# Two feed-forward stages of a four-layer gated transformer: bfloat16 terms without GpSimd, an integer layer's bias as a matrix product, and its rounding issued before attention's last tile

## The chip, the cores and the metric

The kernel runs on one core of a Trainium2 chip. The core has five engines, which run side by side and wait for each other through semaphores: TensorE (PE; its weight loads are shown apart as PEld), VectorE (DVE), ScalarE (ACT), GpSimd (POOL) and SyncE (SP), which here only issues DMAs. Data lies in SBUF, and matrix products arrive in PSUM.

The metric is the device time of one execution, in microseconds, as the median of several. A profile is one such execution with a record of every instruction. Its span is the time from the first instruction to the last.

## The reference

The input x has 4 x 256 tokens of 256 features. Four layers follow each other, each with an attention over a context of 64 rows and a feed-forward part. Either part adds `tanh(gate) * f(layernorm(x))` to x. The two feed-forward parts that matter here are those of layers 1 and 2:

```python
def _L1_ffn_ref(x, w1, b1, w2, b2):
    w1_q = absmean_quant(w1)                    # values -1, 0, 1
    w2_q = absmean_quant(w2)
    h = jnp.einsum('bsd,fd->bsf', x, w1_q) + b1           # 256 -> 1024
    h = jax.nn.gelu(h, approximate=False)
    out = jnp.einsum('bsf,df->bsd', h, w2_q) + b2         # 1024 -> 256
    return out

def _L2_ffn_ref(x, weight, bias):
    w_max = jnp.clip(jnp.max(jnp.abs(weight), axis=1, keepdims=True), 1e-08, None)
    w_scale = w_max / QMAX                                # QMAX = 127
    w_q = jnp.clip(jnp.round(weight / w_scale), QMIN, QMAX).astype(jnp.int8)
    w_scale = w_scale.squeeze(1).astype(jnp.float32)
    x_max = jnp.max(jnp.abs(x), axis=2, keepdims=True)
    x_scale = jnp.maximum(x_max / QMAX, 1e-12)
    x_q = jnp.clip(jnp.round(x / x_scale), QMIN, QMAX).astype(jnp.int8)
    acc = jnp.einsum('bnd,od->bno', x_q.astype(jnp.int32), w_q.astype(jnp.int32))
    y = acc.astype(jnp.float32) * x_scale.astype(jnp.float32) * w_scale[None, None, :]
    y = y + bias
    return y.astype(x.dtype)
```

Layers 0 and 3 have mixtures of experts as their feed-forward parts, and the attentions differ from layer to layer.

## The kernel before

The 1024 tokens are 8 tiles of 128 (`NT`), taken in 2 groups of 4 (`NG`, `TPG`). A group's 512 tokens are one moving operand of a product. x stays in SBUF for the whole kernel, as `stream`, with one view `x[t]` a tile. Eight steps run in order: attention and feed-forward of layer 0, then 1, 2 and 3.

The code issues instructions to the five engines, and each engine works its own list in order. The lists aren't quite in the order of the code. When the program is built, a scheduler puts an instruction forward that would be ready earlier by its own reckoning, and takes the order of the code as priority. In the trace, VectorE clears a tile of the last step (L1002) at 695.74 us, while attention of layer 2 still runs. So moving a call in the code moves its priority, and only with it its place.

Buffers come from pools by tag. PSUM has four single-bank tiles (`ps_mm`, tag `mm`) and two double ones (`ps_wide`). Of the normalised tiles (tag `xn`) there are six, which attention's small context copies share.

**Layer 1's feed-forward** (`ffn1`, L1518). The weights are -1, 0 and 1 and exact in bfloat16. The activations are split into three bfloat16 terms whose sum is the float32 value, so each product is done three times in bfloat16. `inputs(g)` (L1524) normalises a group, transposes it and makes its terms, with two casts on ScalarE (L1535, L1537) and two subtractions on VectorE (L1536, L1538) for each half of the features. `up(g)` (L1543) goes through four blocks `f2` of 256 hidden features: 12 products (L1553), two Gelus on ScalarE (L1560), and then `three_terms` (L1479), which splits the block's 128 x 1024 values into three terms. Its four instructions are a cast on ScalarE (L1481), a subtraction on GpSimd (L1482), a cast on VectorE (L1483) and a subtraction on VectorE (L1484). The inputs of group 1 are made ahead of block 2 of group 0. `down(g)` (L1564) takes the terms of all four blocks: 24 products a tile (L1569), the bias (L1577), and the add into x (L456). `in_turn` (L472) issues up 0, up 1, down 0, down 1.

**Layer 2's weights** (`weights2`, L1586) are rounded and transposed before `ffn1` is issued, into `wqT`, 512 columns of a tile with the tag `hits`, which nothing else uses. The gate is multiplied into them there.

**Attention of layers 2 and 3** (`attention23`, L887) runs through `in_flight` (L458), a pipeline of 11 turns over the 8 tiles. In turn i it first lets a side job (`beside`) do one step, then issues the scores of tile i, the add into x of tile i - 3 (`gated_add`, L455), the softmax weights of tile i - 1 (`weights`, L431, a GpSimd multiply), and the attend of tile i - 2 (transposes L451, their evacuations L452, products L953, a context copy L962, products L965). In layer 2 (`keyed`, L974) the side job prepares layer 3's keys and values.

**Layer 2's feed-forward** (`ffn2`, L1613) first loads the bias to all 128 partitions through GpSimd's queue and multiplies the gate into it on GpSimd (L1617). For each group there follow: `layernorm` with the normalisation on ScalarE (statistics L379 and L380, Sqrt L382, normalisation L391), the bias added into the group's four tiles of x on GpSimd (L1622), the largest absolute value of each row (L1626), scale and its inverse (L1627, L1628), rounding to whole numbers on VectorE (L1631, L1632), `transposed` (L400: transposes L406, evacuations L132 and L134), and for each tile two products with `wqT` (L1637) and the add of the product times the row's scale (L456).

`ROUND` is 1.5 x 2^23: adding and subtracting it rounds a float32 to a whole number.

Of the kernel before, what the change touches and what calls it, by code (L numbers as in the profile page):

```python
# [28 lines left out]
F32 = mybir.dt.float32  # L29
# [5 lines left out]
ALU = mybir.AluOpType  # L35
AX = mybir.AxisListType

P = 128
B, S, D = 4, 256, 256
T = B * S  # L40
NT = T // P
TH = 512
NG = T // TH
TPG = TH // P
# [8 lines left out]
ROUND = 12582912.0  # L53
# [28 lines left out]
def tile_flamingo(ctx: ExitStack, tc: tile.TileContext, a: dict, out: bass.AP):  # L82
# [7 lines left out]
    def ps_mm():  # L90
        return psum.tile([P, 512], F32, tag="mm", name="mm", bufs=4)
# [7 lines left out]
    def region(tag, cols, name):  # L99
        return sb.tile([P, cols], F32, tag=tag, name=name, bufs=1)  # L100
# [21 lines left out]
    def small(shape, name, bufs=3):  # L122
        return sb.tile(shape, F32, tag=name, name=name, bufs=bufs)
# [29 lines left out]
    def output_bias(name, src):  # L153

        c = const.tile([P, D], F32, tag="b2", name=name)
        nc.gpsimd.dma_start(out=c[: src.shape[0]], in_=src)
        return c
# [297 lines left out]
    def gated_add(t, ps, gate):  # L455
        nc.vector.scalar_tensor_tensor(x[t], ps, gate, x[t], ALU.mult, ALU.add)  # L456
# [430 lines left out]
    def attention23(layer, gate, beside):  # L887
# [83 lines left out]
        if layer == 3:  # L971
            used("L3")

    def keyed(layer, gate):  # L974
        beside = iter(())
        if layer == 2:
            values = region("wqk", 2048, "values")
            for _ in keys_values(2, region("weff", 2048, "kbd2"), values[:, :1024]):
                pass
            beside = keys_values(3, region("wvo", 2048, "kbd3"), values[:, 1024:])  # L980
        attention23(layer, gate, beside)
        for _ in beside:
            pass
# [492 lines left out]

        return loaded[f"L1_w{k}"][:, :1024].bitcast(BF16)

    def three_terms(terms, v, rest):  # L1479

        nc.scalar.copy(terms[0], v)  # L1481
        nc.gpsimd.tensor_tensor(rest, v, terms[0], ALU.subtract)  # L1482
        nc.vector.tensor_copy(terms[1], rest)  # L1483
        nc.vector.tensor_tensor(terms[2], rest, terms[1], ALU.subtract)  # L1484

    def ternary1():
# [31 lines left out]
    def ffn1(gate):  # L1518
# [23 lines left out]

        def up(g):  # L1543
            for f2 in range(4):
                if g == 0 and f2 == 2:
                    xT.append(inputs(1))
                h = t4([P, 2, TH], "h")
                for j in range(2):
                    f = 2 * f2 + j
                    ps = ps_mm()  # L1550
                    for k, term in enumerate(xT[g]):
                        for c in range(2):
                            nc.tensor.matmul(  # L1553
                                ps,
                                w1[:, c, f * P : (f + 1) * P],
                                term[:, c, :],
                                start=(k == 0 and c == 0),
                                stop=(k == 2 and c == 1),
                            )
                    nc.scalar.activation(h[:, j, :], ps, AF.Gelu, bias=b1_1[:, f : f + 1])  # L1560
                three_terms([hidden[:, g, k, 2 * f2 : 2 * f2 + 2, :] for k in range(3)], h, h)
            return hidden[:, g]

        def down(g, terms):  # L1564
# [21 lines left out]
    def weights2(gate):  # L1586
# [13 lines left out]
            nc.vector.tensor_scalar(q, q, ROUND, 127.0, ALU.subtract, ALU.min)  # L1600
            nc.vector.tensor_scalar(q, q, -128.0, ws[:, c : c + 1], ALU.max, ALU.mult)
        nc.vector.tensor_scalar(wq, wq, gate, None, ALU.mult)
        wqT = sb.tile([P, 768], F32, tag="hits", name="wqT", bufs=1)[:, :512].rearrange("p (d o) -> p d o", d=2)
        ps = ps_mm()
        for d in range(2):
            for c in range(2):
# [1 line left out]
                    ps[:, d * D + c * P : d * D + (c + 1) * P], wq[:, c, d * P : (d + 1) * P], ident  # L1608
                )
        nc.scalar.copy(wqT.rearrange("p d o -> p (d o)"), ps)  # L1610
        return wqT

    def ffn2(gate):  # L1613
        bias_2 = output_bias("bias_2", a["L2_bias"].partition_broadcast(P))
        used("L2")
        wqT = kept.pop("weights2")
        nc.gpsimd.tensor_tensor(bias_2, bias_2, gate.to_broadcast([P, D]), ALU.mult)  # L1617
        for g in range(NG):
            xn = layernorm(g, True)

            tiles = stream[:, g * TPG : (g + 1) * TPG, :]
            nc.gpsimd.tensor_tensor(tiles, tiles, bias_2.unsqueeze(1).to_broadcast([P, TPG, D]), ALU.add)  # L1622
            xs = small([P, TPG], "xs")
            xi = small([P, TPG], "xi")
            for i, n in enumerate(xn):
                nc.vector.tensor_reduce(xs[:, i : i + 1], n, AX.X, ALU.max, apply_absolute_value=True)  # L1626
            nc.vector.tensor_scalar(xs, xs, 1.0 / 127.0, 1e-12, ALU.mult, ALU.max)  # L1627
            nc.vector.reciprocal(xi, xs)  # L1628
            for i, n in enumerate(xn):

                nc.vector.tensor_scalar(n, n, xi[:, i : i + 1], 127.0, ALU.mult, ALU.min)  # L1631
                nc.vector.tensor_scalar(n, n, ROUND, ROUND, ALU.add, ALU.subtract)  # L1632
            xqT = transposed(xn)
            for i in range(TPG):
                ps = ps_mm()
                for d in range(2):
                    nc.tensor.matmul(  # L1637
                        ps[:, :D], xqT[:, d, i * P : (i + 1) * P], wqT[:, d, :], start=(d == 0), stop=(d == 1)
                    )
                gated_add(g * TPG + i, ps[:, :D], xs[:, i : i + 1])  # L1640

    steps = [
        attention0,
# [156 lines left out]
```

## Time and profile before

| | |
|---|---|
| median of 3 runs | 962.89 us (954.0 to 962.95) |
| the profiled execution | 967.09 us |
| its span, first to last instruction | 965.3 us |
| granted TensorE clock, mean over the span | 0.941 |
| attention of layer 1 ends, layer 1's feed-forward begins on TensorE (L1533) | 575.4 us |
| its products up (L1553) | 576.73 to 610.38 us |
| its products down (L1569) | 610.38 to 632.42 us |
| attention of layer 2, its last product (L965) ends | 704.30 us |
| products of layer 2's feed-forward (L1637) | 711.21 to 724.08 us |

Two notes on reading. An instruction's line is that of the helper that issues it: every add into x is L456, whatever stage it belongs to, and only the time tells them apart. A float32 product appears as two records, a bfloat16 one as one. In the timeline, a number in brackets is the idle time of the engine ahead of a row, with the instruction that ended it.

### The profile page before, as it was taken

How to read it: one execution, taken by the hardware profiler on the slowest of the kernel's cores; microseconds unless marked ns; L12 is line 12 of the kernel's file. 1: busy time of each engine (PE TensorE's matmuls, PEld its weight loads, DVE VectorE, ACT ScalarE, POOL GpSimd, SP SyncE). 2: the span in 40 equal slices, each digit the busy share in tenths (PEclk: the TensorE clock that was granted, in tenths of full speed). 3: DMA queues.
4: the chain of work that ended last, by engine and by line, in shares of the span. 5: the costliest groups of instructions: out<-in, count | busy, mean ns of one | idle time of the engine just before them, and what ended most of it. 6: DMA issues, size and time to landing. Idle time of an engine off the chain costs nothing.

```text
span 965.3 us, 12724 instructions
## 1 busy us (share of the span) xinstructions
PE 856.9 (89%) x4467; PEld 555.5 (58%) x4467; DVE 509.9 (53%) x1299; ACT 286.8 (30%) x559; POOL 345.7 (36%) x262
## 2 busy tenths in 40 slices
PE   6999999999999999986199986997867889999994
PEld 4444336876667876764046872754544556666662
DVE  4566648748624444571427755867776856222220
ACT  2122014433112322322113445415534441122221
POOL 1454543110146787786001323402311302144421
PEclk9999999999779999998599999986988999999998
DMA  9201157000256666655640000360000012122223
GB/s 364 79 21 34 61 160 200 22 22 9 84 129 158 125 141 150 121 82 63 186 174 1 1 1 0 111 227 1 1 22 1 1 44 54 43 45 45 39 23 66
DMA packets 38762, 75.15 MB, mean 78 GB/s; under 512 B 6240, under 2 KB 26706, under 8 KB 37322
## 3 DMA queue, kind: packets, MB, share of 16 engines
q1 hardware_dynamic: 23562, 52.01, 16.0%
q0 software_dynamic: 14496, 20.47, 13.1%
q10 hardware_dynamic: 640, 1.84, 0.5%
q8 instruction: 39, 0.64, 0.3%
q14 instruction: 25, 0.20, 0.1%
HBM read 58.73 MB, written 16.61 MB: 78 GB/s over the span
## 4 chain that ended last, share of the span: by engine, by line
PE 31%; DVE 10%; issue 4%; ACT 3%; POOL 2%; DMA 0%; POOLq 0%; ACTq 0%; DVEq 0%
PE wide L1226 7%; PE mm L421 5%; PE mm L1250 3%; PE wide L1436 2%; PE mm L451 2%; PE mm L656 2%; PE mm L965 2%; PE wide L923 1%; PE mm L1457 1%; DVE mx L934 1%; DVE attn L936 1%; PE mm L1637 1%; PE mm L1241 1%; DVE big L1483 1%; POOL h L1482 1%
## 5 line engine op out<-in xcount | busy, mean ns | idle before, releaser
L437 POOL TENSOR_TENSOR attn<-attn,sm 128x1024 f32<-128x1024 f32 x32 | 60.9, 1903 | 212.5 <-DVE sm L436 192.5
L1235 DVE SCALAR_TENSOR_TENSOR blk<-wide,weight,blk 128x176 f32<-128x176 f32 (+1 forms) x75 | 37.0, 493 | 135.3 <-ACT blk L1234 121.2
L1262 POOL DMA_INDIRECT sums<-ring,big x55 | 88.1, 1601 | 33.6 <-issue 10.2
L421 PE MATMUL wide<-xT,big 128*128 128x512 f32 x192 | 86.7, 600 | 0.3 <-ACT big L556 0.3
L683 DVE TENSOR_TENSOR rope<-wide,big 128x512 f32<-128x512 f32 x96 | 59.6, 683 | 47.7 <-PE wide L421 46.6
L1174 POOL DMA_INDIRECT xs<-xd,big x55 | 54.9, 999 | 63.3 <-DMA sums<-x 35.6
L1215 PE MATMUL wide<-big,blk 128*128 x220 | 77.1, 472 | 0.0
L1226 PE MATMUL wide<-big,blk 128*128 x160 | 72.2, 593 | 0.5 <-DVE blk L1187 0.5
L1234 ACT ACTIVATE blk<-wide 128x176 f32<-128x176 f32 (+1 forms) x75 | 29.4, 392 | 122.3 <-PE wide L1226 60.2
L421 PEld LDWEIGHTS wide<-xT,big 128*128 128x128 f32 x192 | 35.0, 190 | 46.7 <-issue 40.5
L656 PE MATMUL mm<-vo,attnT 128*128 128x256 f32 x256 | 59.5, 386 | 0.9 <-ACT attnT L452 0.9
L1250 PE MATMUL mm<-big,blk 88*128 x220 | 57.4, 383 | 0.6 <-ACT blk L1243 0.5
L406 PE MATMUL mm<-ident,xn 128*128 128x128 f32 x112 | 19.4, 320 | 41.6 <-DVE xn L394 35.5
L656 PEld LDWEIGHTS mm<-vo,attnT 128*128 128x128 f32 x256 | 48.0, 193 | 9.1 <-ACT attnT L452 3.1
L456 DVE SCALAR_TENSOR_TENSOR x<-mm,tg,x 128x256 f32<-128x256 f32 x48 | 22.9, 478 | 54.9 <-PE mm L656 17.3
L1250 PEld LDWEIGHTS mm<-big,blk 88*128 88x128 f32 x220 | 41.9, 192 | 16.5 <-ACT blk L1243 1.5
L452 ACT COPY attnT<-mm 128x512 f32<-128x512 f32 x64 | 35.0, 588 | 54.6 <-PE mm L451 54.3
L1215 PEld LDWEIGHTS wide<-big,blk 128*128 128x128 f32 x220 | 40.6, 196 | 13.2 <-issue 1.3
L451 PE MATMUL mm<-ident,attn 128*128 128x128 f32 x256 | 38.0, 297 | 9.9 <-POOL attn L437 9.9
L435 DVE TENSOR_REDUCE sm<-attn 128x16 f32<-128x1024 f32 x32 | 38.8, 1212 | 14.9 <-ACT attn L429 12.4
L1174 POOL DMA_INDIRECT xs<-xd,scratch x20 | 19.5, 976 | 74.6 <-PE mm L1186 53.9
L1262 POOL DMA_INDIRECT sums<-ring,scratch x20 | 31.5, 1573 | 39.3 <-ACT ring L1261 16.8
(321 smaller groups left out, 1698.6 us busy)
## 6 DMA issues: line engine op xcount, KB each, us to landing
big<-in_L_w_gate_up SPq DMA_DIRECT2D x8, 1024.0 KB
big<-in_L_w SPq DMA_DIRECT2D x4, 1408.0 KB
big<-in_L_w_down SPq DMA_DIRECT2D x8, 512.0 KB
w_L_qk<-in_L_qk SPq DMA_DIRECT2D x4, 896.0 KB
big<-in_L_w SPq DMA_DIRECT2D x4, 704.0 KB
big<-in_L_wo SPq DMA_DIRECT2D x1, 2048.0 KB
xd<-xn SPq DMA_DIRECT2D x16, 128.0 KB
sums<-x SPq DMA_DIRECT2D x16, 128.0 KB
```

The costliest lines, as they stand in the source:

```text
L421: nc.tensor.matmul(ps, w(c), xT[:, c, :], start=(c == 0), stop=(c == 1))
L435: nc.vector.tensor_reduce(sm, e, AX.X, ALU.add)
L437: nc.gpsimd.tensor_tensor(e, e, sm.unsqueeze(2).to_broadcast([P, groups, n]), ALU.mult)
L451: nc.tensor.transpose(ps[:, i * P : (i + 1) * P], ev[:, pr * P : (pr + 1) * P], ident)
L656: nc.tensor.matmul(ps[:, :D], aT[:, s, :], vo[:, s, :], start=(s == 0), stop=(s == NP - 1))
L683: nc.vector.tensor_tensor(m[:, s, :].rearrange("q (b t) -> q b t", t=S), ps[:, s, :].rearrange("q (b t) -> q b t", t=S), table, ALU.mult,)
L1174: nc.gpsimd.indirect_dma_start(out=xs, out_offset=None, in_=self.xd, in_offset=bass.IndirectOffsetOnAxis(ap=self.gather[:, b : b + 1].bitc ...
L1215: nc.tensor.matmul(ps[:, 0, : 2 * n], st[:, c * P : (c + 1) * P], self.w[:, bass.ds(r + c * 2 * n, 2 * n)], start=False, stop=(c == 1),)
L1226: nc.tensor.matmul(ps[:, k, :n], st[:, c * P : (c + 1) * P], self.w[:, bass.ds(r + (2 * c + k) * n, n)], start=(c == 0), stop=(c == 1),)
L1235: nc.vector.scalar_tensor_tensor(s, lin, self.weight.pop(b), s, ALU.mult, ALU.mult)
L1250: nc.tensor.matmul(ps[:, :D], hT[:, j * P : (j + 1) * P], self.w[: self.chunk, bass.ds(r + j * D, D)], start=(j == 0), stop=(j == self.n - 1),
L1262: nc.gpsimd.indirect_dma_start(out=self.sums[b % len(self.sums)], out_offset=bass.IndirectOffsetOnAxis(ap=self.scatter[:, b : b + 1].bitca ...
```

## The change

There are three edits.

1. `three_terms` does its first subtraction on VectorE instead of GpSimd. A new argument says which engine makes the second term: VectorE in the even blocks, ScalarE in the odd ones. The inputs of group 1 are made ahead of block 1 of group 0, not block 2.
2. Layer 2's bias is loaded as one row by SyncE's queue when the weights are prepared, into the columns of the weights' tile that were free, and VectorE multiplies the gate into it. In the feed-forward, a product of a row of ones with that row begins each tile's sum in PSUM. The two GpSimd adds into x, the GpSimd multiply, and the load to all partitions are gone.
3. Normalising and rounding become a function of their own, `rounded(g)`. Its rounding multiplies the row's scale back in, instead of clipping at 127, so the last add has no scale. `rounded(0)` is called in turn 9 of attention's pipeline, ahead of the add of tile 6, of the attend of tile 7 and of the add of tile 7. A generator `beside2` around the side job does this. `rounded(1)` stays where it was.

```diff
+    def beside2(keys):
+        for i in range(NT + 3):
+            if i == NT + 1:
+                kept["rounded"] = rounded(0)
+            next(keys, None)
+            yield
+
     def keyed(layer, gate):
...
-            beside = keys_values(3, region("wvo", 2048, "kbd3"), values[:, 1024:])
+            beside = beside2(keys_values(3, region("wvo", 2048, "kbd3"), values[:, 1024:]))
         attention23(layer, gate, beside)
...
-    def three_terms(terms, v, rest):
+    def three_terms(terms, v, rest, scalar):

         nc.scalar.copy(terms[0], v)
-        nc.gpsimd.tensor_tensor(rest, v, terms[0], ALU.subtract)
-        nc.vector.tensor_copy(terms[1], rest)
+        nc.vector.tensor_tensor(rest, v, terms[0], ALU.subtract)
+        (nc.scalar.copy if scalar else nc.vector.tensor_copy)(terms[1], rest)
         nc.vector.tensor_tensor(terms[2], rest, terms[1], ALU.subtract)
...
             for f2 in range(4):
-                if g == 0 and f2 == 2:
+                if g == 0 and f2 == 1:
                     xT.append(inputs(1))
...
-                three_terms([hidden[:, g, k, 2 * f2 : 2 * f2 + 2, :] for k in range(3)], h, h)
+                three_terms([hidden[:, g, k, 2 * f2 : 2 * f2 + 2, :] for k in range(3)], h, h, f2 % 2 == 1)
...
-        wqT = sb.tile([P, 768], F32, tag="hits", name="wqT", bufs=1)[:, :512].rearrange("p (d o) -> p d o", d=2)
+        kept_2 = sb.tile([P, 768], F32, tag="hits", name="kept_2", bufs=1)
+        wqT = kept_2[:, :512].rearrange("p (d o) -> p d o", d=2)
...
-        return wqT
+        bias_2 = kept_2[:1, 512:]
+        nc.sync.dma_start(out=bias_2, in_=a["L2_bias"].partition_broadcast(1))
+        nc.vector.tensor_scalar(bias_2, bias_2, gate[:1], None, ALU.mult)
+        return wqT, bias_2
+
+    def rounded(g):
+
+        xn = layernorm(g, True)
+        xs = small([P, TPG], "xs")
+        xi = small([P, TPG], "xi")
+        for i, n in enumerate(xn):
+            nc.vector.tensor_reduce(xs[:, i : i + 1], n, AX.X, ALU.max, apply_absolute_value=True)
+        nc.vector.tensor_scalar(xs, xs, 1.0 / 127.0, 1e-12, ALU.mult, ALU.max)
+        nc.vector.reciprocal(xi, xs)
+        for i, n in enumerate(xn):
+            nc.vector.tensor_scalar(n, n, xi[:, i : i + 1], ROUND, ALU.mult, ALU.add)
+            nc.vector.tensor_scalar(n, n, ROUND, xs[:, i : i + 1], ALU.subtract, ALU.mult)
+        return xn

     def ffn2(gate):
-        bias_2 = output_bias("bias_2", a["L2_bias"].partition_broadcast(P))
         used("L2")
-        wqT = kept.pop("weights2")
-        nc.gpsimd.tensor_tensor(bias_2, bias_2, gate.to_broadcast([P, D]), ALU.mult)
+        wqT, bias_2 = kept.pop("weights2")
         for g in range(NG):
-            xn = layernorm(g, True)
-
-            tiles = stream[:, g * TPG : (g + 1) * TPG, :]
-            nc.gpsimd.tensor_tensor(tiles, tiles, bias_2.unsqueeze(1).to_broadcast([P, TPG, D]), ALU.add)
-            xs = small([P, TPG], "xs")
-            xi = small([P, TPG], "xi")
-            for i, n in enumerate(xn):
-                nc.vector.tensor_reduce(xs[:, i : i + 1], n, AX.X, ALU.max, apply_absolute_value=True)
-            nc.vector.tensor_scalar(xs, xs, 1.0 / 127.0, 1e-12, ALU.mult, ALU.max)
-            nc.vector.reciprocal(xi, xs)
-            for i, n in enumerate(xn):
-
-                nc.vector.tensor_scalar(n, n, xi[:, i : i + 1], 127.0, ALU.mult, ALU.min)
-                nc.vector.tensor_scalar(n, n, ROUND, ROUND, ALU.add, ALU.subtract)
-            xqT = transposed(xn)
+            xqT = transposed(kept.pop("rounded") if g == 0 else rounded(g))
             for i in range(TPG):
+                t = g * TPG + i
                 ps = ps_mm()
+                nc.tensor.matmul(ps[:, :D], ones[:1], bias_2, start=True, stop=False)
                 for d in range(2):
                     nc.tensor.matmul(
-                        ps[:, :D], xqT[:, d, i * P : (i + 1) * P], wqT[:, d, :], start=(d == 0), stop=(d == 1)
+                        ps[:, :D], xqT[:, d, i * P : (i + 1) * P], wqT[:, d, :], start=False, stop=(d == 1)
                     )
-                gated_add(g * TPG + i, ps[:, :D], xs[:, i : i + 1])
+                nc.vector.tensor_tensor(x[t], ps[:, :D], x[t], ALU.add)
```

## The prediction

> **What bounds the kernel now.** I read the page first, then the chain of waits in order of time, then the groups by shape, the waits and the timeline of the two places that the change touches.
>
> ```profile
> PE 856.9 (89%) x4467; PEld 555.5 (58%) x4467; DVE 509.9 (53%) x1299; ACT 286.8 (30%) x559; POOL 345.7 (36%) x262
> ...
> PE 31%; DVE 10%; issue 4%; ACT 3%; POOL 2%; DMA 0%; POOLq 0%; ACTq 0%; DVEq 0%
> ```
>
> TensorE is nearly always occupied, so what an edit is worth is TensorE's idle time (and its slowed time) in the edited stretch. The chain passes through layer 1's feed-forward by way of GpSimd L1482 and VectorE L1483/L1484 from 587.38 to 622.86 us. The stretches there, and those of layer 2's feed-forward, are these (columns: length, busy time of PE, PEld, DVE, ACT and POOL, granted TensorE clock, DMA):
>
> ```profile
> 584.20:592.79 8.59, 4.69 (x24) 2.16 (x23) 3.25 (x3) 5.56 (x10) 4.21 (x2) 0.97 0.00 0
> 592.79:603.91 11.12, 8.09 (x30) 3.27 (x30) 8.49 (x9) 5.54 (x8) 4.21 (x2) 0.87 0.00 0
> 603.91:610.38 6.47, 6.47 (x30) 2.93 (x30) 2.69 (x3) 6.00 (x10) 3.08 (x2) 1.00 0.00 0
> 610.38:621.78 11.40, 10.65 (x97) 9.39 (x96) 11.30 (x9) 3.91 (x5) 6.74 (x3) 1.00 0.25 75
> ...
> 704.30:711.21 6.91, 1.96 (x8) 1.43 (x8) 6.08 (x19) 2.20 (x6) 2.34 (x1) 0.80 0.22 76
> 711.21:724.10 12.89, 10.75 (x42) 8.48 (x43) 10.02 (x38) 4.40 (x9) 2.34 (x1) 0.84 0.00 0
> ```
>
> The up phase of layer 1 runs from 576.73 to 610.38, the down phase from there to 632.42. The waits and the groups by shape of that stage name the cause:
>
> ```profile
> L1482 POOL TENSOR_TENSOR h<-h,big 128x1024 f32<-128x1024 f32 x8 | 18.2, 2304 | 29.4 <-PE mm L1533 17.9 <-PE mm L1553 5.8 <-ACT big L1481 5.7
> ...
> L1483 DVE CAST big<-h 128x1024 bf16<-128x1024 f32 x8 | 13.1, 1642 | 13.2 <-POOL h L1482 13.2
> L1484 DVE TENSOR_TENSOR big<-h,big 128x1024 bf16<-128x1024 f32 x8 | 11.6, 1446 | 0.2
> L1560 ACT ACTIVATE h<-mm,fixed 128x512 f32<-128x512 f32 x16 | 10.4, 697 | 6.0 <-PE mm L1553 6.0
> ...
> L1481 ACT CAST big<-h 128x1024 bf16<-128x1024 f32 x8 | 8.5, 1057 | 0.1
> ```
> ```profile
> PE mm L1553 <- DVE more L1536: 4.6, 2, 3.4
> ...
> PE mm L1553 <- DVE more L1538: 3.0, 1, 3.0
> ```
>
> The second group's input terms (L1536, L1538) queue on VectorE behind casts (L1483) that take up to 2.61 us beside a GpSimd subtraction and 0.68 us alone. TensorE stands from 589.35 to 592.79 (3.44) and from 600.88 to 603.91 (3.03), and the matmuls from 592.79 to 597 run at a granted clock of 0.65, some 1.9 us lost. With 0.76 at 621 that is 9.1 us of removable time after 584.20.
>
> The timeline at layer 2's feed-forward:
>
> ```profile
> 703.01 2.07 ACT L391 ACTIVATE xn<-x,shift,rstd 128x256 f32<-128x256 f32 x4
> 703.16 0.73 PEld L965 LDWEIGHTS mm<-w_L,ctxTok 128*128 128x128 f32 x4 [0.76 <-ACT ctxTok L962]
> ...
> 706.05 1.48 DVE L1627 TENSOR_SCALAR xs<-xs 128x4 f32<-128x4 f32 x1
> ...
> 708.74 1.96 PE L406 MATMUL mm<-ident,xn 128*128 128x128 f32 x8 [4.44 <-DVE xn L1632]
> ...
> 711.21 5.69 PE L1637 MATMUL mm<-wqT,xT 128*128 128x256 f32 x16 [0.52 <-ACT xT L132]
> ...
> 720.36 3.72 PE L1637 MATMUL mm<-wqT,xT 128*128 128x256 f32 x16 [0.57 <-ACT xT L132]
> ```
>
> Attention's last product ends at 704.30. Normalising, scaling and rounding of group 0 all come after it, so TensorE waits 4.44 us, and then the same sixteen records take 5.69 instead of 3.72.
>
> **Part 1, layer 1's terms.** Removed: eight GpSimd subtractions (18.2 us). Added on VectorE: eight subtractions of the shape of L1484, at 1.22 undisturbed. Moved: four of the eight second casts from VectorE (0.68) to ScalarE (1.05, the row of L1481). Two groups of four blocks then cost:
> - VectorE: 8 x (1.22 + 1.22) + 4 x 0.68 + inputs of group 1, 4 x 0.69 = 25.0 us. Before, the rows of L1483 and L1484 with the same inputs sum to 27.4, plus 13.2 of waiting.
> - ScalarE: 16 Gelus (two in 1.28, so 0.64) + 8 x 1.05 + 4 x 1.05 + 4 x 0.60 = 25.2 us. TensorE: 96 matmuls at 0.216 = 20.7 us.
>
> So VectorE and ScalarE, not TensorE, pace the up phase after the edit, at 2.8 to 2.9 us a block against 2.6. The inputs of group 1 are issued one block sooner, their 8 transposes, 4 casts and 4 subtractions with them. VectorE has idled from 582.66 to 589.54, and with one block fewer ahead of them their PSUM tiles need not wait for a Gelu (they did at 585.21). Their third term should be there by about 592, not 603.85. Walking ScalarE on from the first Gelu at 584.47: six blocks at 2.86 plus 2.4 of input casts gives 604.0; allowing 0.5 for order, the up phase ends at 604.5 instead of 610.38. VectorE starts at 586.8 and has 25.0 us of work and some 2.9 of gaps: the last term is there at 614.7. The first down pass ends at 604.5 + 10.64 = 615.1, so the second doesn't wait, and ends at 625.8 against 632.42: 6.6 us. TensorE carries this to the next stage, whose key products came directly at 632.35. Bounds: 9.1, if neither engine paces; 2, if most gaps return. I take 6.5.
>
> **Part 2, bias and rounding of layer 2.** Removed: the broadcast DMA of the bias and a multiply on GpSimd (633.22 to 641.93, beside other work), two GpSimd adds of 2.34, and VectorE's small scaling at 706.05 that took 1.48 beside the first of them and 0.16 in group 1. Added with the weights: a 1 KB DMA on SyncE's queue, which issues nothing between 482.55 and 610.58, so it lands long before; and a multiply of one row on VectorE, queued with the weights' operations at 571 to 572.9, where VectorE had idled 3.69 us and does again: at most 0.3 us, and nothing in the sum. [...] The final scaled add becomes a plain add of the same kind (0.48 to about 0.41).
>
> Added on TensorE: eight bias products, of one row by 256 columns. None of one row is in the trace; the four 64-row records of L860 hold TensorE for 0.97 us, 0.24 each, and the sixteen 128-row ones at 720.36 for 3.72, 0.233 each, so fewer rows save nothing. A product is two records, 0.465: 1.9 us a group. Below, it is nothing where they run ahead of xT in TensorE's waits; above, 0.71 at the slow clock of 711.21. I take 0.465.
>
> Moved: group 0's layer norm (statistics, one Sqrt, 4 ScalarE normalisations of 0.52), 4 maxima, 2 small operations and 8 roundings on VectorE (4 x 0.55), from behind attention to ahead of the last tile's attend. They pass the last tile's transposes' evacuations on ScalarE (1.07), its context copy and two adds into x. No DMA is among them. ScalarE idles in 694.8 to 695.3 and 699.4 to 701.1, VectorE mostly from 698.2: shift is ready at 698.15, the normalisations fit into 698.5 to 701.2 with at most 0.5 us lost by the last evacuation, and the rounding ends at about 704. Transposes (1.04) and evacuation (0.6) follow attention's last product at 704.3: products start at 706.0 instead of 711.21. At full clock they take 5.6 with the bias, to 711.6. Group 1's chain starts from the last tile's add (704.8): statistics to 706.2, normalisation and maxima to 708.9, rounding to 711.1, and about 1 us for group 0's adds in between: transposed at 712.2, products from about 713 to 718.6, less some bias products that fit in the waits. That is 719 instead of 724.08: 5 us. Bounds: 7 and 1.
>
> **Two rules against this part.** The first row: the eight products at 711.21 at a granted 0.65, after 6.9 us of little work. [...] I expect about 1.7 us of waiting and take the full clock.
>
> The second: a Sqrt issued sooner may fall between two Exps. The table load costs 1.28 (695.72), and the Sqrt began directly after it, at 697.02. [...] I add none: the last Exp starts at 692.52, and the statistics that Sqrt needs end at 695.64, after it.
>
> **Sum.** 6.5 + 5.0 = 11.5 us off the profiled execution's 967.09 (span 965.3 and 1.8 around it): 955.6, a factor of 0.988. The median of the runs is 962.89, 0.4% below that execution, so I say 951.4. The range of the three runs (954.0 to 962.95) is as large as the gain; a change of under 1% (9.6 us) can't be told from none.
>
> **Rivals.**
> - Half of part 1 comes back: ScalarE and VectorE, at 25 us each, wait for each other (sum of both chains per block is longer than either), and the up phase ends near 608.5. Part 1 gives 2.5, part 2 4.5 to 5: about 955.5. For it: both have more work than TensorE. Against: neighbouring blocks are independent, and the trace of before shows their instructions interleaved. 0.15.
> - Part 2 gives little: the moved rounding is placed on the engines where it was, or the clock stays low, and 3.7 us of bias products eat the rest. 0 to 1.5 from it: about 955.7. For it: the order on each engine isn't that of the code (fills of L1002 run at 695.74, far ahead of their stage). 0.10.
> - Slower: on ScalarE, which works in order, each odd block's second cast waits for VectorE's subtraction, and the Gelu queued behind it, TensorE's PSUM release, waits too. Three such casts stand ahead of the Gelus that the last up products need, so a stall S costs 3 S. From S = 3.8 us on it takes all 11.5. A full block of VectorE ahead of the subtraction (3.1 + 1.2 = 4.3) gives 12.9: 964.3 us, and with one more cast in the way 966. Against: VectorE isn't that far behind, at equal loads. 0.07.
>
> **How the numbers follow.** The forecast has 0.68, and about four fifths of it lie beyond 1%: 0.55 for faster. Two rivals (6 to 7.5 us) and the rest give 0.38 within 1%. For slower by over 1%, 0.07 covers the stall and what I have not seen. The range goes from both best bounds with the lower run of before (16 us, and some of 9) at 943 to a gain of 4 at 959.
>
> **What would show it.** No GpSimd work in layer 1's up phase; second casts at 0.68; no TensorE gap over 3 us there and no clock of 0.65; up phase about 28 us long, not 33.7. Roundings of group 0 before attention's last product ends; first products of layer 2 within 2 us of it; from there to the last of them 14 to 15 us instead of 19.8. Wrong if Gelus stand behind waiting casts, or if the products after attention take more than 0.6 us each.

## The result, and the profile after

The kernel after takes 959.08 us (median of 20 runs, 947.34 to 964.35), the kernel before, run beside it, 961.53 us (20 runs, 954.0 to 970.67). The ratio is 0.9933, with a 95% interval of 0.9908 to 0.9957: 6.4 us less. Ratios, here and below, compare fast runs alone, which leaves out the six of the 20 runs after that took over 961.5 us, and so the gain is larger than the 2.45 us between the medians of all runs. The forecast was 1.2%, 11.5 us. The direction was right, the size about half. Set against the 962.89 us shown before, the ratio makes 956.4 us, inside the forecast's range of 943 to 959. It is less than the 1% below which the prediction saw no change that can be told from none, though its interval lies clear of 1.

The profiled execution of the kernel after took 959.15 us, its span is 957.4. The first lines of the page and the shares of the chain of waits:

```profile
PE 860.9 (90%) x4480; PEld 558.1 (58%) x4483; DVE 508.9 (53%) x1304; ACT 290.1 (30%) x563; POOL 319.9 (33%) x250
...
PE 38%; DVE 7%; ACT 3%; POOL 1%; issue 1%; DMA 1%; POOLq 0%; ACTq 0%; DVEq 0%
```

GpSimd lost 26 us of work, and the chain goes less through VectorE and "issue" than before. TensorE is busy for 4 us *more*, though 6 us were won: the first sign that something was added to the bounding engine. A split of the span by stage shows where it went (ffn1 runs from layer 1's first input transpose to its last down product, "layer 2's stage" from attention's last product to the end of the last product of the feed-forward; us):

| profile | before ffn1 | ffn1 | attention 2 | layer 2's stage | the rest | span |
|---|---|---|---|---|---|---|
| before | 575.4 | 57.0 | 71.9 | 19.8 | 241.2 | 965.3 |
| after | 570.0 | 47.9 | 70.0 | 23.8 | 245.6 | 957.4 |

The first column is work that the change doesn't touch. It differs by 5.4 us, mainly because the granted clock between 240 and 300 us was 0.80 in the one execution and 0.94 in the other, and it mustn't be read as gain. Of the other stages, layer 1 gave 9.1 us, more than the 6.5 forecast; layer 2's stage, from which 5.0 were to come, got 4.0 us *longer*; and the work behind it another 4.4.

Layer 1, as stretches of time (length, busy time of PE, PEld, DVE, ACT and POOL, granted clock, DMA). The up phase ends at 596.8, the first down pass is the third row, the second the fourth; the last two rows are layer 2's two groups of products, told of below:

```profile
580.00:590.00 10.00, 9.95 (x46) 4.55 (x47) 8.78 (x10) 10.00 (x15) 0.00 (x0) 1.00 0.00 0
590.00:596.80 6.80, 6.76 (x32) 3.01 (x32) 6.77 (x8) 6.74 (x10) 0.00 (x0) 1.00 0.00 0
596.80:607.40 10.60, 10.59 (x98) 9.50 (x98) 10.53 (x17) 5.81 (x7) 0.00 (x0) 1.00 0.26 67
607.40:617.90 10.50, 10.50 (x98) 9.23 (x95) 6.61 (x20) 0.30 (x1) 0.00 (x0) 1.00 0.83 295
687.95:696.80 8.85, 7.33 (x34) 4.68 (x31) 7.61 (x28) 2.96 (x6) 0.00 (x0) 0.99 0.19 61
696.80:711.75 14.95, 14.70 (x33) 8.53 (x34) 5.64 (x19) 2.85 (x6) 0.00 (x0) 0.50 0.00 0
```

In the first four rows TensorE has hardly a gap left and its clock is 1.00 throughout. ScalarE is full up to 596.8, VectorE nearly so up to 607.4, into the first down pass, and neither holds TensorE up. Its longest waits there, and the groups by shape of the same stage:

```profile
PE mm L1560 <- ACT xT L1544: 1.7, 1, 1.7
...
PE mm L1560 <- ACT h L1567: 0.5, 1, 0.5
```
```profile
L1567 ACT ACTIVATE h<-mm,fixed 128x512 f32<-128x512 f32 x16 | 10.3, 701 | 0.0
L1489 DVE TENSOR_TENSOR h<-h,big 128x1024 f32<-128x1024 f32 x8 | 9.6, 1218 | 0.0
L1491 DVE TENSOR_TENSOR big<-h,big 128x1024 bf16<-128x1024 f32 x8 | 9.5, 1219 | 0.0
...
L1490 ACT CAST big<-h 128x1024 bf16<-128x1024 f32 x4 | 4.2, 1055 | 2.9 <-DVE h L1489 2.9
L1490 DVE CAST big<-h 128x1024 bf16<-128x1024 f32 x4 | 2.8, 694 | 0.1
```

The waits of 3.4 and 3.0 us for the second group's input terms are gone. The casts take 0.69 us undisturbed, the subtractions 1.22, as priced. Of ScalarE's four second casts only the last waits for VectorE, for 2.9 us from 600.3 on, and no Gelu is left behind it. TensorE's wait of 0.5 us for a Gelu is that for the first ones, ahead of all of these casts (579.96).

TensorE's timeline in layer 2's feed-forward (L1646 is the bias product, L1648 the two products with the weights; start, length, idle time before and what ended it):

```profile
689.89 1.99 PE L1648 MATMUL mm<-kept,xT 128*128 128x256 f32 x8
691.81 0.69 PE L1646 MATMUL mm<-kept,ones 1*128 1x256 f32 x2
692.44 1.13 PE L1648 MATMUL mm<-kept,xT 128*128 128x256 f32 x4
693.50 0.69 PE L1646 MATMUL mm<-kept,ones 1*128 1x256 f32 x2
...
696.77 0.69 PE L406 MATMUL mm<-ident,xn 128*128 128x128 f32 x2 [1.52 <-DVE xn L1635]
...
705.38 1.22 PE L1646 MATMUL mm<-kept,ones 1*128 1x256 f32 x2
706.52 2.08 PE L1648 MATMUL mm<-kept,xT 128*128 128x256 f32 x4
708.53 1.22 PE L1646 MATMUL mm<-kept,ones 1*128 1x256 f32 x2
```

Attention's last product ended at 687.95, and the first products start 1.94 us later, not 6.9: the early rounding works. But from the short wait before 696.77 on, every record takes about twice as long. The windows above say the same: 0.99 in the first stretch and 0.50 in the second, though TensorE is then busy for 14.70 of 14.95 us. A tile with its bias takes 1.69 us in the first stretch (691.81 to 693.50) and 3.15 in the second (705.38 to 708.53).

### The profile page after: what moved, and what is told of

Same layout as the page of the kernel before. It is cut to its first block, busy times and chain, and to the rows that moved or that the text cites. A ratio compares the mean times of both kernels' runs of the same rounds, so it can differ in the third digit from the quotient of the medians.

```text
span 957.4 us, 12740 instructions
## 1 busy us (share of the span) xinstructions
PE 860.9 (90%) x4480; PEld 558.1 (58%) x4483; DVE 508.9 (53%) x1304; ACT 290.1 (30%) x563; POOL 319.9 (33%) x250
## 4 chain that ended last, share of the span: by engine, by line
PE 38%; DVE 7%; ACT 3%; POOL 1%; issue 1%; DMA 1%; POOLq 0%; ACTq 0%; DVEq 0%
PE wide L1233 7%; PE mm L421 5%; PE mm L1257 3%; PE wide L1443 2%; PE mm L656 2%; PE mm L1576 2%; PE mm L1560 2%; PE mm L451 2%; PE mm L965 2%; PE wide L923 1%; PE mm L1464 1%; PE mm L1648 1%; PE mm L406 1%; DVE mx L934 1%; DVE attn L936 1%; ACT attnT L452 1%
## 5 line engine op out<-in xcount | busy, mean ns | idle before, releaser
L406 PE MATMUL mm<-ident,xn 128*128 128x128 f32 x112 | 20.6, 331 | 35.4 <-DVE xn L394 33.8
L1222 PEld LDWEIGHTS wide<-big,blk 128*128 128x128 f32 x220 | 41.5, 199 | 13.6 <-issue 1.7
L1233 PEld LDWEIGHTS wide<-big,blk 128*128 128x128 f32 x160 | 28.8, 190 | 28.9 <-issue 28.2
```

What stands on the lines that cost most here:

```text
L1222: nc.tensor.matmul(ps[:, 0, : 2 * n], st[:, c * P : (c + 1) * P], self.w[:, bass.ds(r + c * 2 * n, 2 * n)], start=False, stop=(c == 1),)
L1233: nc.tensor.matmul(ps[:, k, :n], st[:, c * P : (c + 1) * P], self.w[:, bass.ds(r + (2 * c + k) * n, n)], start=(c == 0), stop=(c == 1),)
```

## The experiments

Ten more kernels were run, and two of the kernels profiled once more. Their profiles by stage, as above, with the ratio of their times to the kernel before:

| profile | ffn1 | attention 2 | layer 2's stage | the rest | ratio (95%) |
|---|---|---|---|---|---|
| before | 57.0 | 71.9 | 19.8 | 241.2 | |
| after | 47.9 | 70.0 | 23.8 | 245.6 | 0.9933 (0.9908 to 0.9957) |
| p1_only | 47.9 | 69.9 | 20.4 | 240.3 | 0.9879 (0.9845 to 0.9914) |
| p2_only | 57.0 | 67.6 | 23.8 | 245.2 | 1.0056 (1.0033 to 1.0078) |
| no_product | 48.6 | 69.8 | 16.8 | 240.9 | 0.9880 (0.9852 to 0.9908) |
| full_rows | 49.0 | 68.4 | 14.9 | 243.9 | 0.9885 (0.9855 to 0.9915) |
| rows_32 | 48.6 | 65.4 | 20.1 | 241.3 | 0.9893 (0.9856 to 0.9931) |
| f16_rows | 47.9 | 70.0 | 17.0 | 241.8 | 0.9891 (0.9854 to 0.9927) |
| early_pool | 47.9 | 70.1 | 19.9 | 240.3 | 0.9914 (0.9879 to 0.9949) |
| late_full | 49.6 | 68.6 | 19.8 | 242.9 | 0.9919 (0.9890 to 0.9949) |
| p1_inputs | 53.5 | 68.0 | 20.5 | 241.0 | 0.9962 (0.9944 to 0.9979) |
| p1_terms | 49.4 | 68.2 | 20.6 | 241.2 | 0.9923 (0.9890 to 0.9956) |
| after_again | 47.9 | 69.7 | 23.8 | 245.3 | profile alone, 965.2 us |
| full_again | 49.6 | 68.7 | 14.9 | 244.9 | profile alone, 950.41 us |

**Each part alone.** p1_only has the edits of layer 1 on the kernel before, p2_only those of layer 2.

```diff
 p1_only, on before:
-        nc.gpsimd.tensor_tensor(rest, v, terms[0], ALU.subtract)
-        nc.vector.tensor_copy(terms[1], rest)
+        nc.vector.tensor_tensor(rest, v, terms[0], ALU.subtract)
+        (nc.scalar.copy if scalar else nc.vector.tensor_copy)(terms[1], rest)
...
-                if g == 0 and f2 == 2:
+                if g == 0 and f2 == 1:
...
 p2_only, on after: the same lines undone
```

> Layer 1's edits alone, layer 2 as before. In the profile of the changed kernel layer 1's feed-forward lasted 47.9 us from its first transpose to its last product, against 57.0 before. If layer 1 carries the whole gain and layer 2's edits lose: stage 47 to 49 us, total 8 to 9 us below before, so a ratio near 0.991, at or below the changed kernel's 0.9933. If both parts gain (as forecast): stage the same, but the ratio stays above 0.9933, near 0.995.

> Layer 2's edits alone, layer 1 as before. If layer 2's edits lose because TensorE runs at half clock in them: the stage from attention's last product to the last product of layer 2's feed-forward lasts 22 to 24 us against 19.8 before, granted clock near 0.5 for over 10 us, ratio 1.002 to 1.005. If the half clock in the one profile was chance: 16 to 18 us in this profile, ratio 0.995 to 0.998.

Layer 1's edits alone gain 1.21% (11.6 us of 961.19; 9.4 by the medians). Layer 2's alone *lose* 0.56% (5.4 us). The product of the two ratios is 0.9934, the change's own 0.9933: within the intervals the parts add up, and the change is a gain with a loss in it. In p1_only's profile the up phase (585 to 601) and the two down passes (601 to 622) are filled by TensorE to the last hundredth of a us:

```profile
585.00:595.00 10.00, 10.00 (x48) 4.54 (x47) 9.79 (x11) 9.97 (x15) 0.00 (x0) 1.00 0.00 0
595.00:601.00 6.00, 6.00 (x30) 2.80 (x29) 5.97 (x7) 5.97 (x8) 0.00 (x0) 1.00 0.00 0
601.00:622.00 21.00, 21.00 (x193) 18.66 (x191) 16.96 (x37) 5.89 (x8) 0.00 (x0) 1.00 0.56 184
```

p2_only has the same half clock as after:

```profile
706.50:721.50 15.00, 14.69 (x33) 8.52 (x34) 5.73 (x20) 2.85 (x6) 0.00 (x0) 0.50 0.00 0
```

**The bias product left out, and with all rows at work.** no_product computes layer 2's feed-forward without its bias. full_rows loads the bias into 128 rows, divides it by 128, and multiplies with 128 rows of ones, so that the same number of products is issued.

```diff
 no_product:
-                nc.tensor.matmul(ps[:, :D], ones[:1], bias_2, start=True, stop=False)
 full_rows:
-        bias_2 = kept_2[:1, 512:]
-        nc.sync.dma_start(out=bias_2, in_=a["L2_bias"].partition_broadcast(1))
-        nc.vector.tensor_scalar(bias_2, bias_2, gate[:1], None, ALU.mult)
+        bias_2 = kept_2[:, 512:]
+        nc.sync.dma_start(out=bias_2, in_=a["L2_bias"].partition_broadcast(P))
+        nc.vector.tensor_scalar(bias_2, bias_2, gate, 1.0 / P, ALU.mult, ALU.mult)
...
-                nc.tensor.matmul(ps[:, :D], ones[:1], bias_2, start=True, stop=False)
+                nc.tensor.matmul(ps[:, :D], ones, bias_2, start=True, stop=False)
```

> The changed kernel without the eight one-row bias products (layer 2's bias is left out of the computation). They hold 16 records, 3.7 us at full clock, 7.4 at half. If the products of one row keep the array's clock shut (little activity counted): clock back at 1.00 within about 4 us of group 1's products, stage 15 to 16 us, total 6 to 8 us below the changed kernel. If the clock falls for the wait ahead of group 1 alone: the half clock stays in the first 3 to 6 us of group 1, and the total is 2 to 4 us below the changed kernel.

> The changed kernel with the bias product over all 128 rows (bias / 128 in every row, ones in all rows): the same sum, the same columns and records, 128 times the active rows. If one-row products keep the clock shut: clock 1.00 again within about 4 us in group 1, total 4 to 7 us below the changed kernel. If rows don't matter: the same as the changed kernel within 2 us, half clock from about 697 to 713 us.

TensorE's instructions in full_rows stand in the same order as in after; only the rows at work differ. The stage falls from 23.8 to 14.9 us. Its timeline and its two windows:

```profile
692.76 0.59 PE L1646 MATMUL mm<-kept,ones 128*128 128x256 f32 x2
693.20 1.03 PE L1648 MATMUL mm<-kept,xT 128*128 128x256 f32 x4
694.06 0.59 PE L1646 MATMUL mm<-kept,ones 128*128 128x256 f32 x2
...
697.30 0.44 PE L406 MATMUL mm<-ident,xn 128*128 128x128 f32 x2 [1.79 <-DVE xn L1635]
```
```profile
689.39:697.30 7.91, 6.13 (x33) 5.01 (x30) 7.30 (x28) 2.96 (x6) 0.00 (x0) 1.00 0.22 68
697.30:704.25 6.95, 6.49 (x33) 5.49 (x34) 5.64 (x19) 2.86 (x6) 0.00 (x0) 1.00 0.00 0
```

A tile takes 1.30 us (692.76 to 694.06) against 1.69 with one row, both at full clock. From start to start, the bias product of 128 rows takes 0.44 us (692.76 to 693.20) and the four records after it 0.86 (to 694.06). Taken off the 1.69, these 0.86 leave 0.83 as what a bias product of one row costs its tile. And the wait before group 1, at 1.79 us even longer than after's 1.52, leaves the clock at 1.00. no_product, with no products to fill its wait, shows a third case:

```profile
694.92 3.72 PE L1647 MATMUL mm<-kept,xT 128*128 128x256 f32 x16 [0.56 <-ACT xT L132]
701.66 2.16 PE L406 MATMUL mm<-ident,xn 128*128 128x128 f32 x8 [3.02 <-DVE xn L1635]
704.29 5.92 PE L1647 MATMUL mm<-kept,xT 128*128 128x256 f32 x16 [0.46 <-ACT xT L132]
```

There the wait is 3.02 us, and the sixteen records behind it take 5.92 instead of 3.72. By the trace's record of the granted clock this half clock lasts from 701.96 to 708.78, 6.8 us; that of after lasts from 696.57 to 713.64, 17.1 us, past the end of the stage.

**Other numbers of rows.** rows_32 spreads the bias over 32 rows. f16_rows splits it into three float16 terms over 96 rows, so that a bias product is one record, not two. Of their edits only the added lines are shown.

```diff
 rows_32:
+        bias_2 = kept_2[:32, 512:]
+        nc.sync.dma_start(out=bias_2, in_=a["L2_bias"].partition_broadcast(32))
+        nc.vector.tensor_scalar(bias_2, bias_2, gate[:32], 1.0 / 32, ALU.mult, ALU.mult)
...
+                nc.tensor.matmul(ps[:, :D], ones[:32], bias_2, start=True, stop=False)
 f16_rows:
+        bias_2 = kept_2[:96, 512:640].bitcast(F16)
+        rest = sb.tile([P, 512], F32, tag="low", name="rest", bufs=1)[:96, :D]
+        nc.sync.dma_start(out=rest, in_=a["L2_bias"].partition_broadcast(96))
+        nc.vector.tensor_scalar(rest, rest, gate[:96], 1.0 / 32, ALU.mult, ALU.mult)
+        nc.vector.tensor_copy(bias_2, rest)
+        for rows in (slice(32, 64), slice(64, 96), slice(64, 96)):
+            nc.vector.tensor_tensor(rest[rows], rest[rows], bias_2[rows], ALU.subtract)
+            nc.vector.tensor_copy(bias_2[rows], rest[rows])
...
+                nc.tensor.matmul(ps[:, :D], ones16[:96], bias_2, start=True, stop=False)
```

> The bias product over 32 rows (bias / 32 in each) in place of one row or 128. If the clock counts how much of the array works: a quarter of the rows is between the two, either like 128 rows (stage from attention's last product to layer 2's last product near 15 us, ratio near 0.9885) or like one row (23.5 us, ratio near 0.9933); the profile's clock after the wait ahead of group 1 tells which. If the long half clock with one row was chance: clock and time don't follow the rows, and this is anywhere between.

> The bias in three float16 terms in three bands of 32 rows, one product of one record a tile instead of two: eight records at about 0.11 us, so 0.9 us of bias instead of 3.7, with 96 rows active. If part 2 is worth its 5 us once the clock stays open: stage 13 to 15 us, ratio 0.983 to 0.987, faster than layer 1's edits alone (0.9879). If the products are also what keeps the array busy in the wait ahead of group 1: less of it, half clock for 3 to 6 us, and ratio near 0.988.

First rows_32's timeline, then that of f16_rows:

```profile
691.22 0.69 PE L1646 MATMUL mm<-kept,ones 32*128 32x256 f32 x2
...
692.90 0.69 PE L1646 MATMUL mm<-kept,ones 32*128 32x256 f32 x2
...
696.17 0.44 PE L406 MATMUL mm<-ident,xn 128*128 128x128 f32 x2 [1.52 <-DVE xn L1635]
```
```profile
696.80 0.27 PE L1651 MATMUL mm<-kept,ones 96*128 96x256 f16 x1
696.91 1.03 PE L1653 MATMUL mm<-kept,xT 128*128 128x256 f32 x4
697.77 0.27 PE L1651 MATMUL mm<-kept,ones 96*128 96x256 f16 x1
...
701.70 0.44 PE L406 MATMUL mm<-ident,xn 128*128 128x128 f32 x2 [2.79 <-DVE xn L1640]
```

With 32 rows a tile takes as long as with one (691.22 to 692.90, 1.68 us). The wait is after's, 1.52 us, but the half clock lasts 6.8 us instead of 17.1: the stage is 20.1 us. One 96-row record costs only some 0.1 us (a tile takes 0.97); the wait is then longer, 2.79 us, and the half clock behind it 6.8 us again. The length of the slow stretch with the same instructions and the same order thus goes with the rows at work: 17.1 us with 1, 6.8 with 32, none with 128.

The traces allow a closer look. In all fourteen, up to TensorE's last product, the granted clock changes only at the ends of steps of 3.41 us (17.1 us are five steps, 6.8 two). Two such steps of after, and one of full_rows (columns as above):

```profile
693.16:696.57 3.41, 2.09 (x8) 0.97 (x7) 2.91 (x14) 0.00 (x0) 0.00 (x0) 1.00 0.00 0
703.40:706.81 3.41, 3.41 (x8) 1.83 (x8) 1.92 (x6) 1.14 (x3) 0.00 (x0) 0.50 0.00 0
```
```profile
694.66:698.08 3.42, 1.63 (x9) 1.08 (x9) 3.42 (x17) 0.00 (x0) 0.00 (x0) 1.00 0.00 0
```

Behind the first, with TensorE busy for 2.09 us, the clock falls. In full_rows TensorE is busy for only 1.63 us, the whole wait of 1.79 us lies in the one step, and the clock stays at 1.00. So neither the length of the wait, nor the busy time, nor where the wait falls in a step explains the difference. Without its one-row work (0.62 us, from 693.50 to 694.12) after's step has 1.47 us, and is the emptier of the two. The second step is busy throughout, 1.14 us of it with one row, and the clock stays at 0.50; it is back at 1.00 from 713.64, behind the first step of the stretch that holds no one-row product (710.22 to 713.64). So in these traces the long half clock went with one-row work. By what the clock is granted was not shown, and a fall told of under "What stays open" came behind a step with 128 rows at work.

**GpSimd's adds kept, rounding early; and rounding late with a full bias product.** early_pool takes the bias through GpSimd as before did, but keeps the early rounding. late_full is full_rows without it.

```diff
 early_pool, in ffn2:
+        bias_2 = output_bias("bias_2", a["L2_bias"].partition_broadcast(P))
+        nc.gpsimd.tensor_tensor(bias_2, bias_2, gate.to_broadcast([P, D]), ALU.mult)
...
+            xn = kept.pop("rounded") if g == 0 else rounded(g)
+            tiles = stream[:, g * TPG : (g + 1) * TPG, :]
+            nc.gpsimd.tensor_tensor(tiles, tiles, bias_2.unsqueeze(1).to_broadcast([P, TPG, D]), ALU.add)
...
-                nc.tensor.matmul(ps[:, :D], ones[:1], bias_2, start=True, stop=False)
 late_full, on full_rows:
-            beside = beside2(keys_values(3, region("wvo", 2048, "kbd3"), values[:, 1024:]))
+            beside = keys_values(3, region("wvo", 2048, "kbd3"), values[:, 1024:])
...
-            xqT = transposed(kept.pop("rounded") if g == 0 else rounded(g))
+            xqT = transposed(rounded(g))
```

> The changed kernel with the bias added on GpSimd as before (broadcast load, multiply, two adds of 2.34 us) and no bias products; the early rounding stays. If GpSimd's adds were worth removing: VectorE's work in group 1 stretches by 1 to 2 us, stage 17 to 18 us against 16.7 without any bias. If the bias product was the only cost: stage near 16.7, ratio near 0.988, better than the changed kernel's 0.9933.

> The 128-row bias product, but group 0's normalising and rounding issued in the feed-forward itself, after attention. If moving it earlier is what shortens the stage: TensorE waits 3 to 4.5 us again after attention, stage 18 to 20 us, ratio 0.992 to 0.994 (0.9885 with it moved). If the scheduler would have put it early in any case: stage near 15 us, ratio near 0.9885.

By the stage, early rounding is worth 4.9 us (19.8 with late_full, 14.9 with full_rows). Keeping GpSimd's adds costs 3.1 (19.9 against no_product's 16.8), more than either expectation had. The cost shows in early_pool's timeline:

```profile
695.72 2.34 POOL L1643 TENSOR_TENSOR x<-x,bias 128x1024 f32<-128x1024 f32 x1 [7.95 <-ACT xn L391]
...
696.58 1.50 DVE L1628 TENSOR_SCALAR xs<-xs 128x4 f32<-128x4 f32 x1
...
699.46 2.16 PE L406 MATMUL mm<-ident,xn 128*128 128x128 f32 x8 [4.44 <-DVE xn L1632]
```

A scaling of four numbers a row takes 1.50 us beside the GpSimd add and ends with it (698.08 and 698.06), everything behind it on VectorE is late, TensorE waits 4.44 us, and the sixteen records of group 1 then take 6.30. In the timed ratios neither difference can be told from none: the intervals overlap.

**Layer 1's two edits apart.** p1_inputs only makes the second group's inputs one block sooner, p1_terms only takes the terms off GpSimd. after_again and full_again are second profiles of after and full_rows.

```diff
 p1_inputs, on before:
-                if g == 0 and f2 == 2:
+                if g == 0 and f2 == 1:
 p1_terms, on before:
-        nc.gpsimd.tensor_tensor(rest, v, terms[0], ALU.subtract)
-        nc.vector.tensor_copy(terms[1], rest)
+        nc.vector.tensor_tensor(rest, v, terms[0], ALU.subtract)
+        (nc.scalar.copy if scalar else nc.vector.tensor_copy)(terms[1], rest)
```

> Only the move of group 1's inputs by one block in layer 1; the first subtraction stays on GpSimd and every second cast on VectorE; layer 2 as before. If the order was the larger fault of the up phase: layer 1's stage near 50 us (57.0 before, 47.9 with both edits), ratio near 0.992. If GpSimd and what it does to VectorE's casts was: stage 53 to 56 us, ratio 0.995 to 0.999.

> Only the new engines for the terms in layer 1, inputs of group 1 where they were; layer 2 as before. If GpSimd and what it does to VectorE's casts was the larger fault: stage 49 to 51 us, ratio 0.990 to 0.993. If the order was: one gap of 3 us and some half clock stay ahead of group 1's products, stage 53 to 55 us, ratio 0.995 to 0.998.

> A second profile of the changed kernel. If one-row products keep the clock shut: half clock again for 14 us or more after the wait ahead of group 1 in layer 2's feed-forward, stage 22 to 24 us. If the first profile was chance: full clock back within about 7 us, stage near 17.

> A second profile of the kernel with the 128-row product. If working rows keep the clock open: half clock for 7 us at most, stage 14.5 to 18 us. If the first profile was chance: a long half clock as with one row, stage 20 us or more.

The sooner inputs give 3.5 us in the stage, the terms 7.6, both together 9.1. So on top of the terms the sooner inputs are worth 1.5 us (49.4 and 47.9, with the clock at 1.00 in both); where the stage takes up to 49.6 with both edits, as in full_rows and late_full, a stretch of half clock lies at its beginning (some 3.4 us in full_rows, 6.8 in late_full). The timed ratios of p1_terms and p1_only can't be told apart. The groups and the longest wait of p1_inputs tell why its edit isn't enough:

```profile
L1482 POOL TENSOR_TENSOR h<-h,big 128x1024 f32<-128x1024 f32 x8 | 19.8, 2480 | 23.2 <-ACT big L1481 19.6 <-PE mm L1553 3.2 <-POOL h L1482 0.5
...
L1484 DVE TENSOR_TENSOR big<-h,big 128x1024 bf16<-128x1024 f32 x8 | 15.2, 1904 | 0.2
L1483 DVE CAST big<-h 128x1024 bf16<-128x1024 f32 x8 | 11.3, 1410 | 1.7 <-POOL h L1482 1.7
```
```profile
PE mm L1553 <- DVE more L1538: 2.9, 1, 2.9
```

VectorE's casts and subtractions still run beside GpSimd's, at 1.41 and 1.90 us instead of 0.69 and 1.22. Of the two long waits of before, that for L1536 is gone and that for L1538 remains with 2.9 us. p1_terms takes the cause away: its longest wait is 1.2 us.

after_again repeats the stage of 23.8 us and the half clock of 17.1 us, full_again the 14.9 us and the clock of 1.00. The long half clock is in all three profiles with one-row products and in neither with 128 rows.

## Why the prediction was half right

The forecast had a gain of 6.5 us from layer 1 and of 5.0 from layer 2. Timed alone, layer 1 gained 11.6 and layer 2 lost 5.4. That the change, with a gain of 6.4, still lies within the forecast's range is luck: an error of 5 us on the one side covers half of an error of 10 on the other.

**Layer 1: the mechanism held, one term was too large.** All signs named but one came: no GpSimd work in the up phase, second casts at 0.69 us, no gap above 3 us, no clock of 0.65. The step that failed is "VectorE and ScalarE, not TensorE, pace the up phase after the edit, at 2.8 to 2.9 us a block". The loads of both were right, but the up phase took 25.4 us (571.35 to 596.8), not 28, because their work needn't end with it. Only the Gelus have to keep up with TensorE. The casts and subtractions behind them trailed into the first down pass: ScalarE's last cast came at 603.2, VectorE's last term at 605.5, still before the second down pass needs it at 607.4. VectorE's last term was worked out at 39.3 us after the stage began and came at 35.5. So the upper bound, 9.1 us, was the result: 9.1 in the stage and 11.6 (8.3 to 14.9, by the ratio's interval) in time. That it fits to the tenth is chance in part, for the bound holds 1.9 us for the slow clock, and 4.21 us at 0.65 lose 1.5. The rival in which the two engines wait for each other did not happen, nor did the stall on ScalarE: no second cast with a Gelu behind it waited at all.

**Layer 2: one half held, the other turned the gain into a loss.** Forecast was a gain of 5.0 us; alone it cost 5.4. The early rounding did what was said: products 1.94 us after attention (1.7 forecast), group 0 in some 5.4 us (5.6, with half of its bias products run ahead), no additional table load (six from 560 to 735 us, as in before). Group 1's transposes came 8.8 us after attention's end, against 7.9. Up to here 0.9 us is missing. Then "At full clock they take 5.6 with the bias" failed for group 1: from its first transpose to the last product 15.0 us passed, where the forecast had 6.8. Two terms make this up:
- "I take 0.465" for a bias product of one row. It costs a tile 0.83 at full clock; 0.465 is about what one of 128 rows costs (0.44). "Fewer rows save nothing" was right, that they cost no more was taken for granted.
- The full clock. That a wait of about 1.7 us leaves it full was the author's estimate, and no run shows it as a rule: behind waits of 1.52 and 1.79 us the granted clock was 0.50 in after and 1.00 in full_rows. For group 0 the estimate held (0.99 from 687.95 to 696.80). In before it fell in the gap of 3.44 us and not behind that of 3.03, and by the steps of 3.41 us the two differ in more than their lengths. The first row below is the step that the longer gap all but fills; the clock fell to 0.50 behind it. The shorter gap is spread over the other two, which kept 1.70 and 2.10 us of TensorE's work, and the clock stayed at 1.00:

```profile
588.94:592.35 3.41, 0.40 (x2) 0.10 (x1) 2.81 (x2) 0.81 (x2) 2.65 (x2) 1.00 0.00 0
599.18:602.59 3.41, 1.70 (x8) 0.69 (x7) 3.15 (x2) 0.17 (x1) 2.27 (x2) 1.00 0.00 0
602.59:606.01 3.42, 2.10 (x10) 0.97 (x10) 3.10 (x4) 1.62 (x3) 0.00 (x0) 1.00 0.00 0
```

In after the clock fell behind a wait of 1.52 us, in a step with 2.09 us of TensorE's work, 0.62 of them with one row. The sum had no price for a slow clock in group 1. It came there, and lasted past the end of the stage (17.1 us). With full_rows the same piece takes 6.95 us (697.30 to 704.25), the 6.8 of the forecast.

The rival "the clock stays low, and 3.7 us of bias products eat the rest" was the nearest, with 0.10. It too was priced too kindly: it ended at a gain of 0 to 1.5.

**What stays open.** full_rows mends layer 2's stage (14.9 us; 14.7 forecast), and yet its ratio, 0.9885, is that of layer 1's edits alone, 0.9879. Both intervals are some 6 us wide, so noise can hide part of the 5.5 us won. In the profiles most of it is given back later: the rest of the span is 243.9 and 244.9 us against p1_only's 240.3. The kernel after pays there too (245.6). Of the 3.6 us that full_rows loses, 1.7 are a dip of the clock in layer 3's shared feed-forward, which from its first product to its last takes 52.9 us in after, p2_only, full_rows, late_full and the two repeats, and 51.2 in the others. In after this dip lasts from 778.49 to 781.90, at 0.50, behind a step in which TensorE was busy throughout (3.41 us), with products of 128 rows, most of them only 8 columns wide. So this fall did not come with few rows at work. Another 1.7 lie in the tail behind TensorE's last product, where the last GpSimd transfer waits longer. That wait in the profile of after, for "issue" where before waited 3.0 us for a DMA:

```profile
POOL sums L1269 <- issue: 5.0, 1, 5.0
```

No run tells what brings either about, and rows_32 and f16_rows show less of it (241.3 and 241.8). No version tried is measurably faster than layer 1's edits alone.

## What to carry to other kernels

An engine with the largest load in a stage needn't pace it: ask which of its instructions the bounding engine waits for, and let the others trail into the next stage, as VectorE's last term did here, 8.7 us past the end of the up phase. A product with one row looked cheap and was not: it cost its tile 0.83 us where one with 128 rows took 0.44, and the clock fell to 0.50 behind it, for 17.1 us. Filling all rows and dividing by their number mended the stage (23.8 to 14.9 us), if not measurably the whole. When a change has two parts, time each alone: here one was worth 1.2% and the other cost 0.6%, which the sum hides.

## What the hardware showed beside this

- The same TensorE instructions in the same order run at a granted clock of 0.50 for 17.1 us with one row of ones in the bias products, and at 1.00 with 128 (three profiles of three, and two of two).
- The granted clock changed only in steps of 3.41 us, in all fourteen traces. A gap of 3.03 us spread over two steps of before left it at 1.00.
- In after TensorE was busy for 14.70 us of the 14.95 from 696.80 on, and the granted clock was still 0.50 at their end.
- A VectorE scaling of 128x4 numbers, 0.16 us alone, ended with the GpSimd add that it met, both times: at 707.53 in before (the add at 707.50) and at 698.08 in early_pool (698.06). Statistics of a tile begun beside the same add, at 696.27, kept their 0.39 us.
- Executions of one kernel spread over 947 to 964 us, and mostly follow the mean granted clock of the whole span, 0.961 down to 0.934. The stretch from 240 to 300 us alone, which the change doesn't touch, moved by 7.5 us between two profiles. Under 1%, stages of a profile have to be compared, not spans.
